# Layer 1's first sum runs behind layer 0's output: the end of a two-layer graph kernel rebuilt

## The chip, the core and the metric

One program runs on one core of a Trainium2 chip. Times are device microseconds (us); the time of the kernel before is the median of three runs, 6874.45 us (6868.21 to 6877.75). One more execution was taken by the profiler, and every line of a profile below comes from that one.

## The reference

Two layers on N = 2708 nodes with 128 features and a dense matrix `adj` (2708 x 2708). Layer 0 is an attention with 128 groups and 8 features in each group: the node matrix `q`, `k`, `v` is read as (128, N, 8), `adj` is added twice to every group's scores, and the softmax goes over the last axis.

```python
a = einsum('dnh,dmh->dnm', q, k) * d ** -0.5
a = softmax(a + adj + adj, axis=2)
out = einsum('dnm,dmh->dnh', a, v).reshape(n, h * d)
x1 = layernorm(x + out @ Wo.T)

local_hidden = adj @ (x1 @ W2) + b2
local_cross = adj @ (local_hidden @ W4) + b4
y = layernorm(x1 + local_cross + local_hidden @ res_w.T + res_b)
```

The `reshape` reads a (128, N, 8) array flat as N rows of 1024 features. 128 rows of the result are therefore 16,384 of the flat (group, node) pairs, some six groups of the attention. The first 128 rows are complete long before the attention ends; only the last ones need its last groups.

## The kernel before

**Attention.** 32 steps of four groups (`GB`), each with six blocks of 452 query nodes (`QB`), each block in nine steps of a `plan`: 1728 steps. TensorE (PE) makes scores and sums weights times values, VectorE (DVE) adds `adj` (L445), ScalarE (ACT) takes exponentials (L536, L539), GpSimd (POOL) multiplies some of them by a stored exponential (L537). A planner, `interleave`, writes the order out by hand. All loads go through SP's DMA queue, eight tiles ahead (`ahead`), from three pools of buffers. `hand_on` (L469 to L471) copies a block's sums out of PSUM and stores them to DRAM (`os`) through the SP queue.

**After it**, `rest(True)` does the remaining work in two stages. A chunk is 128 nodes; there are 22 chunks, the last with 20 nodes. A block is 512 nodes; there are six, the last with 148.

`layer0_out` first loads the weights, then goes over the chunks. Per chunk it loads `ot` (the eight sums and the divisor, 128 x 9 x 128, 576 KB in runs of 512 bytes) and `xt` (the input rows, 64 KB), takes the reciprocal on DVE (L597), notes its smallest and largest value (L600), multiplies (L602), transposes eight 128 x 128 tiles on PE (L605), copies them out on ACT (L607), multiplies them by `wo` (L613, sixteen instructions, since PE makes an f32 product in two passes), and adds `x` with the statistics of the layernorm (L617, L569, L570). `ot` and `xt` have three buffers each; the `xt` of chunk c + 2 waits until chunk c - 1 has been added, and the `ot` of the next chunk stands behind it in SP's queue. After the last chunk, one square root serves all chunks (L632), then every chunk is normalized (L641), transposed (L643) and multiplied by W2 (L651) to give `xw`. A last part, the judgement, checks that sums and exponentials stayed within bounds and puts a number into `n_fine`.

`layer1` runs two passes over the blocks. A pass sums, for each block, 22 products of a chunk of `xw` (then of `hw`) with a 128 x 512 tile of the transposed matrix `adjT`, loaded through SP into 24 buffers (L681, L682). After each block of pass one, the hidden values go to `lhT` (L690) and through W4 to `hw` (L693, L694). After each block of pass two, the residual product is added (L685), the result is transposed, added to `x1`, normalized and stored (L699 to L707).

At the very end the program reads `n_fine`; if the judgement failed, it would do attention and rest again in a slower form. It doesn't here.

[...]A DMA is issued by an instruction on SP's or ACT's queue, and each issue also waits for the DMA that stood eight issues earlier (they share eight completion semaphores).

## Time and profile before

| | us |
|---|---|
| median of three runs | 6874.45 |
| span of the profiled execution, first to last instruction | 6863.4 |
| what lies around the span, by the difference to the median | 11.05 |
| last instruction of the attention's sums on PE ends at | 6522.7 |
| from there to the end | 340.7 |

The profile's own execution is known only by its span. All stages below are read from the span's start. In the stage tables, "busy" is the time in which an engine worked, PEclk the share of full clock that TensorE was granted, and the DMA share the mean busy share of the 16 DMA engines.

### The profile page before, as it was taken

What the parts mean: (1) busy time and instruction counts of PE and PEld (TensorE: products, weight loads), DVE (VectorE), ACT (ScalarE), POOL (GpSimd) and SP (SyncE); (2) the same over time, 40 slices, a digit from 0 to 9 for tenths busy, and PEclk for the clock granted to TensorE, in tenths of its full rate; (3) what the DMA queues carried; (4) which work ended last, traced back from release to release, by engine and by line L of the source; (5) the groups of instructions that cost most, each with busy time, mean ns of one, the idle gap of its engine ahead of it and who ended that gap; (6) DMA issues with size and microseconds to landing.
All of it is one profiled execution on the core that took longest, in us unless ns stands there. A gap on an engine that the chain in (4) does not pass through costs nothing.

```text
span 6863.4 us, 138873 instructions
## 1 busy us (share of the span) xinstructions
PE 6632.4 (97%) x50666; PEld 1992.4 (29%) x50666; DVE 6109.7 (89%) x6373; ACT 6506.3 (95%) x3659; POOL 5788.8 (84%) x2706
## 2 busy tenths in 40 slices
PE   7999999999999999999999999999999999999979
PEld 2222222222222222222222222222222222222254
DVE  6899999999999999999999999999999999999941
ACT  7999999999999999999999999999999999999910
POOL 5899888999988999989889899889999888888800
PEclk8999999999999999999999999999999999999999
DMA  8888888888888888888878778887888787777667
GB/s 263 265 250 248 245 246 249 251 249 247 251 249 248 245 243 247 247 254 254 251 239 249 247 243 250 250 252 242 252 249 244 234 239 235 234 234 231 195 205 232
DMA packets 1168590, 1674.27 MB, mean 244 GB/s; under 512 B 153982, under 2 KB 1135954, under 8 KB 1163802
## 3 DMA queue, kind: packets, MB, share of 16 engines
q1 hardware_dynamic: 1167642, 1664.50, 79.8%
q8 instruction: 402, 6.59, 0.4%
q14 instruction: 290, 2.38, 0.1%
q10 hardware_dynamic: 256, 0.81, 0.1%
HBM read 1582.90 MB, written 81.80 MB: 243 GB/s over the span
## 4 chain that ended last, share of the span: by engine, by line
PE 52%; DMA 12%; DVE 11%; POOL 7%; issue 7%; ACT 6%; SPq 5%; DVEq 0%; POOLq 0%; ACTq 0%
PE acc L463 26%; PE s L438 16%; DVE e L445 9%; POOL w L537 6%; DMA col<-in_adjP 4%; DMA two<-in_adjP 3%; SPq L287 3%; PE acc L682 3%; ACT e L539 3%; ACT w L536 2%; DMA ecol<-ne 2%; PE acc L455 2%; PE p L438 2%; PE s L344 1%; DMA two<-in_adjS 1%
## 5 line engine op out<-in xcount | busy, mean ns | idle before, releaser
L537 POOL TENSOR_TENSOR w<-w,ecol 128x1356 f32<-128x1356 f32 (+1 forms) x1728 | 5347.5, 3102 | 678.8 <-ACT w L536 598.4
L445 DVE TENSOR_TENSOR e<-s,col 128x904 f32<-128x904 f32 (+1 forms) x4608 | 4817.4, 1092 | 306.3 <-PE s L438 68.6
L539 ACT ACTIVATE e<-e 128x2712 f32<-128x2712 f32 (+5 forms) x1728 | 4616.5, 2672 | 17.6 <-DVE e L445 12.0
L463 PE MATMUL acc<-e,vals 128*9 128x452 f32 x20352 | 3554.7, 545 | 0.0
L438 PE MATMUL s<-q,k 32*128 32x452 f32 x10944 | 2492.7, 461 | 122.0 <-DVE e L445 87.7
L536 ACT ACTIVATE w<-p 128x1356 f32<-128x1356 f32 (+1 forms) x1728 | 2308.2, 1336 | 3.0 <-PE p L438 2.5
L438 PEld LDWEIGHTS s<-q,k 32*128 32x128 f32 x10944 | 1002.7, 182 | 3232.8 <-DVE e L445 2845.5
L463 PE MATMUL acc<-w,vals 128*9 128x452 f32 x10368 | 1622.6, 544 | 0.0
L438 PE MATMUL p<-q,k 32*128 32x452 f32 (+1 forms) x5184 | 1322.1, 444 | 25.5 <-ACT w L536 23.1
L445 DVE TENSOR_TENSOR e<-s,two 128x904 f32<-128x904 f32 (+1 forms) x960 | 1049.2, 1093 | 104.5 <-PE s L438 66.0
L463 PEld LDWEIGHTS acc<-e,vals 128*9 128x9 f32 x20352 | 442.3, 88 | 778.0 <-issue 776.5
L438 PEld LDWEIGHTS p<-q,k 32*128 32x128 f32 x5184 | 545.7, 182 | 55.0 <-ACT w L536 47.9
L463 PEld LDWEIGHTS acc<-w,vals 128*9 128x9 f32 x10368 | 209.8, 88 | 176.7 <-issue 159.9
L262 POOL CAST k<-k_raw 128x336 fp32r<-128x336 f32 x251 | 221.6, 883 | 28.2 <-DMA q<-qs 28.2
L460 PE MATMUL acc<-e,v_first 128*32 128x452 f32 (+1 forms) x1536 | 186.7, 558 | 12.8 <-ACT e L539 0.6
L455 PE MATMUL acc<-e,v_short 128*128 128x452 f32 (+1 forms) x384 | 196.7, 594 | 0.0
L344 PE MATMUL s<-wc,xc 128*128 128x256 f32 (+1 forms) x480 | 166.6, 429 | 4.9 <-DMA wc<-in_WqT 0.2
L469 DVE COPY o<-acc 128x452 f32<-128x452 f32 x192 | 120.3, 627 | 51.2 <-PE acc L463 51.2
L360 POOL TENSOR_TENSOR pr<-pa,pr 128x256 fp32r<-128x256 f32 (+1 forms) x160 | 117.5, 734 | 12.8
L346 DVE TENSOR_SCALAR pa<-s 128x256 f32<-128x256 f32 (+1 forms) x240 | 100.4, 419 | 31.1 <-PE s L344 23.7
L344 PEld LDWEIGHTS s<-wc,xc 128*128 128x128 f32 (+1 forms) x480 | 69.5, 183 | 155.0 <-DVE e L445 153.0
L682 PE MATMUL acc<-col,xw 128*128 128x512 f32 (+2 forms) x264 | 105.8, 550 | 0.0
(85 smaller groups left out, 1039.6 us busy)
## 6 DMA issues: line engine op xcount, KB each, us to landing
col<-in_adjP SPq DMA_DIRECT2D x1965, 226.0 KB
two<-in_adjP SPq DMA_DIRECT2D x1440, 226.0 KB
ecol<-ne SPq DMA_DIRECT2D x1395, 226.0 KB
col<-in_adjP SPq DMA_DIRECT2D x393, 224.0 KB
two<-in_adjP SPq DMA_DIRECT2D x288, 224.0 KB
ecol<-ne SPq DMA_DIRECT2D x279, 224.0 KB
col<-in_adjT SPq DMA_DIRECT2D x210, 256.0 KB
k_raw<-ks SPq DMA_DIRECT2D x504, 84.6 KB
```

The lines of the kernel that those rows point to most:

```text
L262: copy(k[:, :, ts(i, n)], t[:, ts(i, n * NU)].rearrange("p (q c) -> p c q", c=NU))
L287: queues[i].dma_start(q[ds(32 * j + 2 * H * i, 2 * H), :nw].bitcast(F32), qs[:, ds((GB * g + j) * N + n0, nw)])
L344: nc.tensor.matmul(pp[:mi, 0, :QW], given[c][:, :mi], given.pop((c, i, h)), start=True, stop=True)
L438: nc.tensor.matmul(to[:, :nw], k[r, m, :], q[r], start=True, stop=True)
L445: nc.vector.tensor_add(e[:, ds(at, 2), :nw], st[:, :, :nw], a)
L455: nc.tensor.matmul(a[:, :nw], vz, e[:, t, :nw], start=False, stop=False)
L460: nc.tensor.matmul(a[ds(32 * j, 32), :nw], v_first[g % 2][:, ds(32 * j, 32)], e[:, t, :nw], start=True, stop=False)
L463: nc.tensor.matmul(a[ds(32 * j, VW), :nw], v[:, m, ds(VW * j, VW)], e[:, t, :nw], start=False, stop=(m == last_chunk))
L536: nc.scalar.activation(w[:, :, :nw], sp[:, :, :nw], AF.Exp, scale=2.0)
L537: nc.gpsimd.tensor_mul(w[:, :, :nw], w[:, :, :nw], exp_cols[g, b, two][:, :nw].unsqueeze(1).to_broadcast([P, 3, nw]))
L539: nc.scalar.activation(e[:, :at, :nw], e[:, :at, :nw], AF.Exp, scale=2.0)
L682: nc.tensor.matmul(acc[:, :nw], src[:mw, m, :], t[:mw, :nw], start=(m == 0), stop=(last is None and m == NM - 1))
```

## The change

The end after the attention is written anew as one function, `finish`; the old form stays only in the part that doesn't run (`again`).

1. Six loads move into the attention: `wo`, the first 128 rows of `adjT` (`near0`), chunk 0's `ot` and `x`, W2 and W4. They are issued on SP's queue at the first six steps of the second block of the last group. The division of chunk 0 (a reciprocal and a multiplication on DVE) goes into the attention's last block.
2. The last store of the attention, and the loads of `rw` and the biases, are issued on ACT's queue.
3. W2 is applied after the sum: adj (x1 W2) becomes (adj x1) W2. Pass one needs only `x1`, so it can start with the first chunk: six accumulators, one for each block, stay open in PSUM, and `spread(c - 2)` adds chunk c - 2 to all six while chunk c is turned and mixed. Each chunk gets its own square root. The rows of `adjT` are loaded whole, 128 x 2708, into six buffers.
4. Two PSUM banks are left for the rest, so transposes are made in two halves through one bank.
5. After the last chunk the sums are taken out, multiplied by W2 (`hidden`) and W4 (`hidden_values`), and pass two (`collect`) begins with the chunks that are ready. Seven of the 22 row chunks are still in SBUF; the other 15 are loaded per block as 128 x 512 tiles into 20 buffers (`fetch`).
6. The output of a block is normalized together (`results`). The judgement runs after the second block of pass two.

```diff
@@ -186,6 +186,15 @@
+    wo = const.tile([P, H, D], F32, name="wo")
+    w2, w4 = (const.tile([P, P], F32, name=f"w{i}") for i in range(2))
+    near0 = const.tile([P, N], F32, name="near0")
+    ot0 = const.tile([P, H + 1, P], F32, name="ot0")
+    x0 = const.tile([P, D], F32, name="x0")
+    o3 = os_.rearrange("e (i g) -> i e g", g=P)
+    early = [(wo.rearrange("g e f -> g (e f)"), WoT), (near0, adjT[:P, :]), (ot0, o3[:P]), (x0, x[:P, :]), (w2, W2), (w4, W4)]
...
@@ -467,8 +476,9 @@
             n0, nw = QBS[b]
             o = opool.tile([P, QB], F32, tag="o", name="o")
             nc.vector.tensor_copy(o[:, :nw], acc.pop((g, b))[:, :nw])
+            queue = nc.scalar if (g, b) == (NG - 1, len(QBS) - 1) else nc.sync
             for j in range(GB):
-                nc.sync.dma_start(os_[:, ds((GB * g + j) * N + n0, nw)], o[ds(32 * j, H + 1), :nw])
+                queue.dma_start(os_[:, ds((GB * g + j) * N + n0, nw)], o[ds(32 * j, H + 1), :nw])
...
@@ -511,6 +521,14 @@
+                if g == NG - 1 and b and early:
+                    nc.sync.dma_start(*early.pop(0))
+                if (g, b) == (NG - 1, len(QBS) - 1) and i in (3, 5):
+                    if i == 3:
+                        quotient = opool.tile([P, QB], F32, tag="o", name="o")[:, :P]
+                        nc.vector.reciprocal(quotient, ot0[:, H, :])
+                    else:
+                        nc.vector.tensor_mul(ot0[:, :H, :], ot0[:, :H, :], quotient.unsqueeze(1).to_broadcast([P, H, P]))
...
-    wo = keep.tile([P, H, D], F32, name="wo")
-    nc.sync.dma_start(wo.rearrange("g e f -> g (e f)"), WoT)
...
-    def layer0_out(sb, ps, pa, judge):
...
-    def layer1(s, cols):
...
+    def finish(s):
+        NR = 6
+        one = s.enter_context(tc.tile_pool(name="one", bufs=1))
+        two = s.enter_context(tc.tile_pool(name="two", bufs=2))
+        sb = s.enter_context(tc.tile_pool(name="end", bufs=3))
+        rpool = s.enter_context(tc.tile_pool(name="rows", bufs=NR))
+        cols = s.enter_context(tc.tile_pool(name="near", bufs=20))
+        turned = s.enter_context(tc.tile_pool(name="turned", bufs=1, space=PSUM))
+        mixed = s.enter_context(tc.tile_pool(name="mixed", bufs=1, space=PSUM))
+        wide = s.enter_context(tc.tile_pool(name="wide", bufs=1, space=PSUM))
+        s.enter_context(tc.manual_schedule())
...
+        given, rows, turns, made, near = {0: (ot0, x0)}, {0: near0}, {}, {}, {}
+        accs = [wide.tile([P, NB], F32, tag=f"acc{k}", name="acc1") for k in range(len(NBS))]
+        def load(c):
+            i0, w = MC[c]
+            ot = sb.tile([P, H + 1, P], F32, tag="ot", name="ot")
+            nc.sync.dma_start(ot[:w], o3[ds(i0, w)])
+            xt = sb.tile([P, D], F32, tag="xt", name="xt", bufs=4)
+            nc.sync.dma_start(xt[:w], x[ds(i0, w), :])
+            given[c] = ot, xt
+        def load_rows(m):
+            m0, mw = MC[m]
+            rows[m] = rpool.tile([P, N], F32, tag="rows", name="rows")
+            nc.sync.dma_start(rows[m][:mw], adjT[ds(m0, mw), :])
+        def divide(c):
+            w, ot = MC[c][1], given[c][0] if c else ot0
+            if c:
+                rd = two.tile([P, P], F32, tag="rd", name="rd")
+                nc.vector.reciprocal(rd[:w], ot[:w, H, :])
+                nc.vector.tensor_mul(ot[:w, :H, :], ot[:w, :H, :], rd[:w].unsqueeze(1).to_broadcast([w, H, P]))
+            for i, op in enumerate((ALU.min, ALU.max)):
+                nc.vector.tensor_reduce(reach[:w, i, c : c + 1], ot[:w, H, :], AX.X, op)
+        def turn(c, h):
+            w, ot = MC[c][1], given[c][0]
+            pt = turned.tile([P, 4, P], F32, tag="pt", name="pt")
+            for e in range(4):
+                nc.tensor.transpose(pt[:, e, :w], ot[:w, 4 * h + e, :], ident[:w, :w])
+            turns[c, h] = two.tile([P, 4, P], F32, tag=f"oT{h}", name="oT")
+            nc.scalar.copy(turns[c, h][:, :, :w], pt[:, :, :w])
+        def mix(c):
+            w = MC[c][1]
+            made[c] = mixed.tile([P, NB], F32, tag="py", name="py")
+            for e in range(H):
+                nc.tensor.matmul(made[c][:w, :D], turns[c, e // 4][:, e % 4, :w], wo[:, e, :], start=(e == 0), stop=(e == H - 1))
+        def add_x(c):
+            w = MC[c][1]
+            y = two.tile([P, D], F32, tag="y", name="y")
+            nc.vector.tensor_add(y[:w], made.pop(c)[:w, :D], given.pop(c)[1][:w])
+            statistics(mvs[:w, c, :], y[:w], w)
+            sd = stat.tile([P, 1], F32, tag="sd", name="sd")
+            nc.scalar.activation(sd[:w], mvs[:w, c, 1:2], AF.Sqrt, bias=eps[:w])
+            rs = stat.tile([P, 1], F32, tag="rs", name="rs")
+            nc.vector.reciprocal(rs[:w], sd[:w])
+            nc.vector.tensor_scalar(x1[:w, c, :], y[:w], mvs[:w, c, 0:1], rs[:w], ALU.subtract, ALU.mult)
+        def spread(m, ks):
+            mw = MC[m][1]
+            for k in ks:
+                n0, nw = NBS[k]
+                nc.tensor.matmul(accs[k][:, :nw], x1[:mw, m, :], rows[m][:mw, ds(n0, nw)], start=(m == 0), stop=(m == NM - 1))
+        NK = len(NBS)
+        resident = {0, *range(NM - NR, NM)}
+        wanted = [(k, m) for k in range(NK) for m in range(NM) if m not in resident]
+        def fetch(n=1):
+            for k, m in wanted[:n]:
+                (n0, nw), (m0, mw) = NBS[k], MC[m]
+                near[k, m] = cols.tile([P, NB], F32, tag="near", name="near")
+                nc.sync.dma_start(near[k, m][:mw, :nw], adjT[ds(m0, mw), ds(n0, nw)])
+            del wanted[:n]
+        for c in (1, 2):
+            load(c)
+            load_rows(c)
+        for t, a in ((rw, res_wT), (b2_sb, b2), (b4_sb, b4), (rb_sb, res_b)):
+            nc.scalar.dma_start(t, a)
+        nrow = 3
+        for c in range(NM):
+            if c + 3 < NM:
+                load(c + 3)
+            while nrow < NM and nrow <= min(c + 4, max(c + NR - 2, NR)):
+                load_rows(nrow)
+                nrow += 1
+            if c == 1:
+                spread(0, range(NK))
+            turn(c, 0)
+            if c > 2:
+                spread(c - 2, range(3))
+            turn(c, 1)
+            if c > 2:
+                spread(c - 2, range(3, NK))
+            mix(c)
+            if c == 0:
+                add_x(0)
+            if c + 1 < NM:
+                divide(c + 1)
+            if c == 0:
+                divide(0)
+            else:
+                add_x(c)
+        fetch(20)
+        nc.vector.tensor_add(bias, b4_sb, rb_sb)
+        spread(NM - 2, range(NK))
...
+        def take(k):
+            nw = NBS[k][1]
+            summed[k] = two.tile([P, NB], F32, tag="summed", name="summed")
+            (nc.vector.tensor_copy if k % 2 else nc.scalar.copy)(summed[k][:, :nw], accs[k][:, :nw])
+        def hidden(k):
+            n0, nw = NBS[k]
+            pl = turned.tile([P, NB], F32, tag="pt", name="pl")
+            nc.tensor.matmul(pl[:, :nw], w2, summed.pop(k)[:, :nw], start=True, stop=True)
+            nc.vector.tensor_scalar(lhT[:, ds(n0, nw)], pl[:, :nw], b2_sb, None, ALU.add)
+        def hidden_values(k):
+            cs = block_chunks[k]
+            ph = mixed.tile([P, 4, P], F32, tag="py", name="ph")
+            for c in cs:
+                m0, mw = MC[c]
+                nc.tensor.matmul(ph[:mw, c - cs[0], :], lhT[:, ds(m0, mw)], w4, start=True, stop=True)
+            full = len([c for c in cs if MC[c][1] == P])
+            nc.scalar.copy(hw[:, ds(cs[0], full), :], ph[:, :full, :])
+            for c in cs[full:]:
+                nc.vector.tensor_copy(hw[: MC[c][1], c, :], ph[: MC[c][1], full, :])
+        def collect(k, ms, first, last):
+            n0, nw = NBS[k]
+            if first:
+                sums2[k] = wide.tile([P, NB], F32, tag=f"acc{NK - 1 - k}", name="acc2")
+            for i, m in enumerate(ms):
+                mw = MC[m][1]
+                t = rows[m][:mw, ds(n0, nw)] if m in resident else near.pop((k, m))[:mw, :nw]
+                nc.tensor.matmul(sums2[k][:, :nw], hw[:mw, m, :], t, start=(first and i == 0), stop=False)
+                fetch()
+            if last:
+                nc.tensor.matmul(sums2[k][:, :nw], rw, lhT[:, ds(n0, nw)], start=False, stop=True)
+        def embed(k):
+            nw = NBS[k][1]
+            embeds[k] = two.tile([P, NB], F32, tag="eT", name="eT")
+            nc.vector.tensor_scalar(embeds[k][:, :nw], sums2.pop(k)[:, :nw], bias, None, ALU.add)
+        def results(k):
+            n0, nw = NBS[k]
+            cs, eT = block_chunks[k], embeds.pop(k)
+            pe = turned.tile([P, 4, P], F32, tag="pt", name="pe")
+            for c in cs:
+                m0, mw = MC[c]
+                nc.tensor.transpose(pe[:mw, c - cs[0], :], eT[:, ds(m0 - n0, mw)], ident)
...
+            for i, n, w in parts:
+                nc.vector.tensor_add(y[:w, ds(i, n), :], pe[:w, ds(i, n), :], x1[:w, ds(cs[0] + i, n), :])
+                for r in range(i, i + n):
+                    statistics(mv[:w, r, :], y[:w, r, :], w)
+                sd, rs = (stat.tile([P, 4], F32, tag=t, name=t) for t in ("sd4", "rs4"))
+                nc.scalar.activation(sd[:w, :n], mv[:w, ds(i, n), 1], AF.Sqrt, bias=eps[:w])
+                nc.vector.reciprocal(rs[:w, :n], sd[:w, :n])
+                for r in range(i, i + n):
+                    nc.vector.tensor_scalar(o[:w, r, :], y[:w, r, :], mv[:w, r, 0:1], rs[:w, r - i : r - i + 1],
+                                            ALU.subtract, ALU.mult)
+                m0 = MC[cs[0] + i][0]
+                nc.sync.dma_start(out[ds(m0, n * w), :].rearrange("(c p) f -> p c f", p=w), o[:w, ds(i, n), :])
+        def judge():
...
+            nc.vector.tensor_reduce(every, fine, AX.X, ALU.min)
...
+            pf = mixed.tile([P, NB], F32, tag="py", name="pf")
+            nc.tensor.matmul(pf[:1, :1], every, ones, start=True, stop=True)
+            nc.vector.tensor_copy(n_fine, pf[:1, :1])
+        spread(NM - 1, [5, 4])
+        take(5)
+        spread(NM - 1, [3])
+        take(4)
+        hidden(5)
+        spread(NM - 1, [2])
+        hidden(4)
+        take(3)
+        spread(NM - 1, [1])
+        hidden_values(5)
+        take(2)
+        spread(NM - 1, [0])
+        hidden_values(4)
+        take(1)
+        order = [*block_chunks[5]]
+        for k in range(3, -1, -1):
+            hidden(k)
+            if k == 1:
+                take(0)
+            collect(0, order, k == 3, False)
+            hidden_values(k)
+            order = [*block_chunks[k + 1]]
+        collect(0, block_chunks[1], False, False)
+        collect(0, block_chunks[0], False, True)
+        embed(0)
+        for k in range(1, NK):
+            collect(k, range(4), True, False)
+            results(k - 1)
+            collect(k, range(4, NM), False, True)
+            embed(k)
+            if k == 1:
+                judge()
+        results(NK - 1)
+    with ExitStack() as s:
+        finish(s)
```

## The prediction

> **What bounds the kernel now.** I first cut the span into stages (busy time by engine), then read the chain that ended last, then the waits of SP's queue. Columns of the stage table: stretch, length, busy time of PE, weight loads, DVE, ACT and POOL, granted clock, DMA share, GB/s.
>
> ```profile
> 6300.00:6520.00 220.00, 207.09 (x1672) 57.85 (x1672) 204.90 (x212) 219.11 (x117) 183.55 (x69) 1.00 0.63 207
> 6522.70:6623.70 101.00, 67.42 (x528) 63.53 (x528) 68.67 (x156) 21.54 (x22) 0.41 (x5) 0.90 0.72 206
> 6623.70:6642.40 18.70, 15.65 (x79) 11.10 (x79) 11.79 (x34) 7.43 (x15) 0.00 (x0) 0.82 0.21 57
> 6642.40:6746.60 104.20, 104.20 (x301) 49.96 (x301) 4.27 (x7) 5.55 (x23) 0.00 (x0) 1.00 0.79 240
> 6746.60:6854.60 108.00, 108.00 (x293) 49.85 (x293) 22.45 (x105) 5.68 (x21) 0.00 (x0) 1.00 0.77 259
> 6854.60:6863.40 8.80, 0.94 (x5) 0.43 (x4) 2.34 (x11) 0.48 (x2) 0.00 (x0) 0.67 0.10 25
> ```
>
> In the attention's last group ACT is busy 219 of 220 us: it sets the pace there. Both passes of layer 1 keep PE busy all the time. Between them and the attention lie 120 us (6522.7 to 6642.4) in which no engine is full. So all that can be gained is in 120 us, about 1.7% of the run.
>
> The chain shows what those 120 us wait for (start, length, what):
>
> ```profile
> 6528.04 4.48 DMA ot<-os
> ...
> 6588.03 0.95 DVE rd L597
> ...
> 6589.31 1.13 DVE on L602
> ...
> 6591.05 4.58 DMA ot<-os
> ...
> 6618.15 0.81 PE pt L605 x8
> 6618.97 3.85 PE py L613 x32
> ...
> 6659.71 0.86 PE acc L682 x2
> ```
>
> Ten microseconds go by between the attention's last sum (6522.7) and the first `ot` (6532.5). Then each chunk costs a load of 4.5 to 5.6 us and some 3 us of DVE, about 7.6 us (6588.03 to the next reciprocal at 6595.65), while the PE needs 0.81 + 3.85/2 = 2.73 us a chunk. SP's waits name the loop: the `xt` load waits for the sums of an older chunk and holds the next `ot` behind it.
>
> ```profile
> SPq L591 <- DVE st L569: 53.3, 19, 4.4
> ```
>
> The chain's last line gives one product of a chunk with a 512-wide block: two passes, 0.86 us.
>
> **The change, part by part.** *PE work* hardly changes. Turn and mix stay at 2.73 us a chunk. Adding a chunk to six sums is 5 x 0.86 + 0.27 (the 148-wide block: 32 instructions took 4.38 us, so 0.27 a pair) = 4.57 us. W2 falls from 22 transposes and 44 products (L643, L651) to five products of 0.86 and one of 0.27, 4.6 us. What changes is that 22 x 4.57 us of pass one lie inside the stage that had holes. If a chunk then costs 2.73 + 4.57 = 7.3 us of PE and nothing else is slower, the stage is PE's.
>
> *Does PE have to wait inside a chunk?* In the built order PE runs: 4 transposes, 3 sums, 4 transposes, 3 sums, 16 mixing products. The second transposes need the one bank copied out by ACT. That copy stands on ACT behind the previous chunk's square root, which waits for DVE: add 0.29, statistics 0.47, root 0.3, copy 0.59 (the 128 x 512 copy at L648), with hops about 1.9 us. PE meanwhile has 0.4 + 2.58 us. The mixing needs the second copy, 0.6 us, behind 1.99 us of sums. DVE per chunk: 0.95 + 1.21 + 0.5 + 0.3 + 0.5 + 0.16 + 0.34 = 4.0 us plus the wait for the root, under 7.3. So none, by about 1 us; if that cover fails, each chunk pays what is missing.
>
> *Do the loads keep up?* A chunk needs 576 + 64 + 1354 KB (128 rows of 10,832 bytes) = 2.04 MB. Nearest rows: 6545 to 6610, mostly `ot`, moved 240 GB/s at a share of 0.82, so 293 when full: 7.0 us. Pass two moved 259 at 0.77, so 336: 6.1 us. [...]The row decides, since a third of the bytes still comes in 512-byte runs: 7.0 us, below 7.3 by little. [...]by the row they set the first four chunks. Below 280 GB/s they set all.
>
> *The start.* ACT's queue now holds, ahead of the first copy of `oT`, eight DMA issues (0.3 to 0.4 us each). They wait for the attention's last sum (6522.7), for DVE's copy (6523.4), and by the shared semaphores for DMAs eight issues back: the fourth store waits for chunk 1's `ot`, issued when POOL ends at 6520.8 and landed 4.5 us later. So the first copy comes at about 6526.4, not 6523.2; queued behind it are all of chunk 0's steps. Then, with hops: copy 0.55, transposes, copy, mixing with a cold clock, add, statistics, root, scale: `x1` of chunk 0 at 6533.6. The timeline shows how PE runs after a hole (start, length of the group, idle time before it in brackets):
>
> ```profile
> 6535.20 1.94 PE L605 MATMUL pt<-ident,on 128*128 128x128 f32 x8 [12.58 <-DVE on L602]
> 6541.43 1.04 PE L605 MATMUL pt<-ident,on 128*128 128x128 f32 x8
> 6550.51 1.94 PE L605 MATMUL pt<-ident,on 128*128 128x128 f32 x8 [2.75 <-DVE on L602]
> ```
>
> Loads come in turn behind each other. The second `ot` waits on a shared semaphore until the first whole row block has landed (6525.5 + 4.5 = 6530), so it lands at about 6534.5; row blocks of about 4.6 us and `ot`s of 2.3 us follow: `ot` 3 at 6541.5, two row blocks, `ot` 4 at 6553.5. Its division takes 2.2 us: chunk 4 starts on PE at about 6556. PE alone would be there at 6553 to 6555, so the loads decide this.
>
> *From there:* 18 chunks x 7.3 = 131.4, less 0.5 for the short last one: 6687. Then two chunks of sums 9.1; W2 4.6; W4 44 products of 0.11 = 4.9; pass two 5 x 23 x 0.86 + 23 x 0.27 = 105.1; transposes of the results 22 x 0.11 = 2.4: together 126.1, to 6813.1. Its tiles: 15 of 22 per block, 3.9 MB in 19.8 us, 200 GB/s against 259 before: hidden, and the first 20 are issued as soon as the last rows are.
>
> *The judgement* moves into pass two. PE's one small product for it stands between the second and third block, and waits for DVE: copy of the sums 0.7, a check on 44 numbers about 0.4, eight small operations and one more 1.4 (6635.95 to 6637.4), hops: PE stands still for 3 us. Queued behind it are the third block's products. SP then reads `n_fine` and holds its loads some 3 us more; by then all 20 buffers are filled, so nothing waits. Does the hole also cool the clock? [...]The third line above shows half speed after 2.75 us of idling, though in a stage with other holes; by that it costs up to 2 more. I take 4.
>
> *In the attention:* the early loads are six issues of about 0.4 us on SP and 2.6 MB, 8 to 9 us of transfer on a share of 0.63; every tile of the second block stands behind them. The table of waits in the last groups shows almost no wait for a load on any engine:
>
> ```profile
> POOL w L537 <- DMA q<-qs: 2.3, 5, 0.5
> ...
> POOL w L537 <- DMA col<-in_adjP: 0.4, 1, 0.4
> ```
>
> Matching issue and first use of each tile, the shortest lead after 6200 is 9.7 us and the median 17, so a delay of 5 is covered; all of it exposed would cost 9. DVE's 0.95 + 1.21 are added at 204.90 busy of 220: 0 to 2.2 us. I take 1 for both. Small waits in the new code: 2. The tail: from the end of PE's last sum to the end of the span was 6863.4 - 6854.6 = 8.8; now DVE also still has the block before to finish: 9.6.
>
> *Sum:* 6813.1 + 1 + 4 + 2 + 9.6 = 6829.7 against 6863.4, that is 33.7 us less, say 34. Against the median: 6874.45 - 34 = 6840, since 11 us around the span stay.
>
> **The rivals.**
>
> *Hidden waits in the chunk.* The margins of about 1 us before the second transposes don't hold, because the chain DVE, ACT, PE crosses three queues. For it: the timeline has hops of 0.1 to 0.2 us between engines, and one late root holds them all. At 0.7 us a chunk: 19 x 0.7 = 13, so 6853.
>
> *The attention pays.* Early loads come in front of its tiles. For it: ACT has no slack (219 of 220), so a late tile is lost time. Against: the leads. At worst 9 + 2.2: 6850.
>
> *Loads keep the pace.* If they stay at the 240 GB/s of the old stage, a chunk costs 8.5 us: 18 x 1.2 + 4 x 1.5 = 28 us of the 34 are lost: 6868, no difference worth naming.
>
> *Slower.* The same place, at a higher price: each `ot` stands on SP's queue behind a row block that waits for a buffer. The gain is gone when 18 (t - 7.3) + 4 (t - 7.0) = 34, so t = 8.8 us a chunk (232 GB/s); it is slower by over 0.2% above 9.4 us. At 10 us: 22 x 10 - 159 = 61 lost, 6901. For it: the old stage moved 206 GB/s on average. Against: it was then SP's waits and not the DMA engines that held it; now an `ot` is asked for three chunks (22 us) ahead.
>
> *Better.* The loads run near 350 GB/s from the start and no clock is lost: 6 to 10 us less, 6832.
>
> **How the numbers follow.** Forecast as worked out (6836 to 6848) 0.56; hidden waits 0.14; the attention pays 0.10; better 0.10; loads keep the pace 0.06; slower 0.04. The range holds the first four: 6828 to 6858, which leaves out 0.10 for the last two and as much for the edges of the others. A difference of 0.2% (13.7 us) is about what a measurement of this kernel can tell from none. Faster: the first four and a third of the fifth, 0.92; same 0.04; slower 0.04.
>
> **What would show it.** Right: the attention's last sum within 2 us of 6522.7; first sum into the accumulators at about 6534, chunk 4 at 6556; from there PE busy all the time with 7.3 us a chunk and clock 1.00; the last sum of pass one near 6700; one hole of 3 us on PE after the second block of pass two; the tail under 10 us. Wrong: a DMA share near 1 with PE below 0.95 in the chunks (loads), transposes waiting for ACT's copy (hidden waits), ACT below 0.99 in the last group (attention).

## The result and the profile after

The changed kernel takes 6854.52 us (median of ten runs, 6848.58 to 6860.71) against 6869.94 us (ten runs of the kernel before, 6865.77 to 6877.75): a ratio of 0.9977, 95% interval 0.9968 to 0.9986. That is 15.4 us less, inside the range on record (6828 to 6858) but less than half of the 34 us forecast; the likeliest case's own range (6836 to 6848) was missed. The profiled span is 6852.6 us, against 6863.4 before: 10.8 us less.

In what follows T0 is the start of the copy of the attention's last sums: 6522.7 before, 6541.05 after. So the attention ended 18.3 us later, and what follows it became 29.1 us shorter (311.6 instead of 340.7). The 18.3 us are 9.4 up to the first block's copy of sums, -1.5 from there to the block before the last group, 3.9 in the next five blocks and 6.6 in the last block.

Two words come back below. A hole is a time in which PE does nothing. A fall is a stretch in which TensorE was granted half of its clock; the trace records the start and length of each.

The stages of the changed kernel, busy time by engine (columns as in the prediction's first table): the attention's last block, the start of `finish`, the chunks, the work up to the second block's end in pass two, the judgement, the rest of pass two, the tail.

```profile
6507.00:6541.00 34.00, 32.36 (x225) 8.12 (x226) 22.69 (x24) 24.42 (x13) 20.77 (x7) 0.80 0.19 59
6541.00:6571.40 30.40, 18.60 (x86) 13.49 (x87) 11.00 (x26) 5.27 (x9) 0.41 (x5) 0.72 0.88 306
6571.40:6708.50 137.10, 137.10 (x685) 89.83 (x683) 68.79 (x167) 25.08 (x57) 0.00 (x0) 1.00 0.80 272
6708.50:6769.70 61.20, 61.15 (x177) 28.41 (x176) 11.49 (x32) 5.35 (x11) 0.00 (x0) 1.00 0.45 134
6769.70:6778.00 8.30, 5.75 (x14) 2.67 (x15) 2.34 (x13) 0.00 (x0) 0.00 (x0) 0.79 0.14 34
6778.00:6842.70 64.70, 64.70 (x190) 31.26 (x188) 16.41 (x59) 1.19 (x4) 0.00 (x0) 1.00 0.43 127
6842.70:6852.60 9.90, 0.46 (x3) 0.15 (x2) 2.77 (x11) 0.59 (x2) 0.00 (x0) 0.61 0.14 42
```

The stage that had holes is PE's now: 137.10 of 137.10 us at full clock with a DMA share of 0.80. Three places are not: the start (18.60 of 30.40), the judgement, and the attention's last block, whose clock fell to 0.80.

The chain that ended last, from the attention's last product on POOL to the first chunk with sums inside (start, length, what):

```profile
6536.01 3.09 POOL w L555
6539.12 4.43 DMA ot<-os
6543.56 5.12 DMA os<-o
6548.71 0.59 ACT oT L636
...
6550.47 3.43 PE py L642 x16
...
6555.91 7.56 PE acc L659 x12
...
6571.35 0.44 PE pt L634 x4
6571.78 2.58 PE acc L659 x6
6574.36 0.44 PE pt L634 x4
6574.80 1.97 PE acc L659 x6
6576.77 1.78 PE py L642 x16
6578.55 0.44 PE pt L634 x4
```

A load, then a store, then the first copy of `oT`, at T0 + 7.7. The chain names the store because it landed last before the copy. What the copy stood behind is seen on ACT's queue:

```profile
6541.05 0.36 ACTq L677 DMA_DIRECT2D rw<-in_res_wT  x1
...
6548.25 0.37 ACTq L677 DMA_DIRECT2D b<-in_res_b  x1
6548.71 0.58 ACT L636 COPY oT<-pt 128x512 f32<-128x512 f32 x1 [10.45 <-DMA os<-o]
```

The last bias waits for the DMA eight issues ahead of it, the load of `rw`: in the trace both tell of their landing by the same one of eight semaphores, and in the profile of before 10,050 of 10,065 issues on SP's queue use the semaphore of the issue eight earlier. By the trace's semaphore records the load of `rw` landed at 6548.23, 7.2 us after its issue; a row block of `adjT`, issued on SP's queue 0.02 us ahead of it, landed at 6548.04. By then the clock is at half (a fall of 17.07 us from 6544.4 on): 3.43 us for the mixing that takes 1.78 later, 7.56 for the first sums instead of 4.55. The last six lines are one chunk as it then repeats: 0.44 + 2.58 + 0.44 + 1.97 + 1.78 = 7.2 us, no idle time between.

SP's waits among the chunks (6560 to 6700):

```profile
SPq L611 <- PE pt L634: 85.1, 18, 6.9
```

An `ot` load now waits for the transposes to free its buffer, that is for PE. Before, it waited for an `xt` load held by the sums.

PE's timeline around the judgement (idle time before the group in brackets):

```profile
6772.25 0.19 PE L792 MATMUL pf<-ones,every 128*1 128x1 f32 x2 [2.60 <-DVE every L789]
6772.37 5.40 PE L741 MATMUL acc<-near,hw 128*128 128x512 f32 x8
```

A hole of 2.6 us, and then eight products in 5.40 us that take 3.60 at full clock (shown below).

### The profile page after: what moved, and what is told of

Its sections match the earlier page's. It is cut to its first block, busy times and chain, and to the rows that moved or that the text cites. A ratio compares the mean times of both kernels' runs of the same rounds, so it can differ in the third digit from the quotient of the medians.

```text
span 6852.6 us, 138413 instructions
## 1 busy us (share of the span) xinstructions
PE 6636.6 (97%) x50612; PEld 1985.7 (29%) x50612; DVE 6114.5 (89%) x6368; ACT 6503.0 (95%) x3660; POOL 5789.9 (84%) x2706
## 4 chain that ended last, share of the span: by engine, by line
PE 51%; DMA 11%; DVE 10%; POOL 9%; issue 7%; ACT 6%; SPq 6%; DVEq 0%; POOLq 0%; ACTq 0%
PE acc L472 25%; PE s L447 16%; DVE e L454 9%; POOL w L555 8%; SPq L296 3%; ACT e L557 3%; DMA col<-in_adjP 3%; DMA two<-in_adjP 3%; ACT w L554 2%; DMA ecol<-ne 2%; PE acc L464 2%; PE p L447 2%; PE acc L659 2%; PE acc L741 2%; PE s L353 1%
## 5 line engine op out<-in xcount | busy, mean ns | idle before, releaser
L659 PE MATMUL acc<-rows,x 128*128 128x512 f32 (+2 forms) x252 | 103.1, 545 | 0.0
```

The lines of the kernel that those rows point to most:

```text
L659: nc.tensor.matmul(accs[k][:, :nw], x1[:mw, m, :], rows[m][:mw, ds(n0, nw)], start=(m == 0), stop=(m == NM - 1))
```

## The experiments

The kernel before was timed again beside each set of runs, with medians of 6865.6 to 6874.5 us. Across sets, therefore, ratios compare better than microseconds.

**Is the late attention a matter of runs?** The copy of sums just before the last group was 7.8 us late already, where nothing had been changed.

> The kernel before, unchanged, profiled once more. The changed kernel's attention ran 7.8 us late already at the end of the block before the last group (6334.05 against 6326.19 for the copy of that block's sums), although the change touches nothing ahead of the last group. If that is a difference from run to run (theory), this profile's copy of the same block may lie anywhere from 6318 to 6342 and the distance from there to the last copy of sums is again 196.5 us to within 1 us. If the change somehow causes it (rival), this profile is within 2 us of 6326.19.

Measured: 6877.72 us, one run. The second profile has this copy at 6338.46, 12 us later than the first and later than the changed kernel's 6334.05. By then its clock had been at half for 27.3 us since block 0, that of the first profile for 3.4. From there to the last copy it takes 199.56 us, not 196.5, with two more falls of 3.4 us each. So the attention as a whole varies by such amounts from run to run, and a single pair of profiles can't tell a few us in it. Its first block is another matter: the first copy of sums stands at 91.19 and 94.43 in the two profiles of before, and at 100.57 after. That is taken up below.

**The division in the last block.**

```diff
             if what == "hand_on":
+                if n == NG * len(QBS) - 1:
+                    quotient = opool.tile([P, QB], F32, tag="o", name="o")[:, :P]
+                    nc.vector.reciprocal(quotient, ot0[:, H, :])
+                    nc.vector.tensor_mul(ot0[:, :H, :], ot0[:, :H, :], quotient.unsqueeze(1).to_broadcast([P, H, P]))
                 hand_on(*divmod(n, len(QBS)))
...
-                if (g, b) == (NG - 1, len(QBS) - 1) and i in (3, 5):
...
```

> The two VectorE instructions that divide chunk 0 (0.94 and 1.22 us) are taken out of the last block and put behind its last addition, ahead of the copy of its sums, where VectorE waits for TensorE anyway. Theory (they stop TensorE, and its clock falls to half afterwards): from the copy of the sums of the last block but one to that of the last takes 27.4 us again as in the kernel before (34.0 in the changed kernel), no slice of the last block has a clock below 0.95, and the whole run is 6 to 7 us shorter than the changed kernel: about 6848, ratio 0.9968 to the kernel before. Rival (the last block suffers from the loads and stores around it): it stays near 34 us with a clock near 0.5 in two stretches, and the time stays at 6854.

Measured: 30.38 us for the last block, 6853.57 us in all (0.9972, 0.9962 to 0.9983). Neither theory's number. One of the two falls of the clock went, the other stayed, behind a hole of 1.06 us that the kernel before has too. The time by itself can't tell this from no change: the interval overlaps that of the changed kernel. The same holds for the experiments on ACT's queue and on the judgement below, which rest on their traces.

The opposite: the division alone, in the kernel before.

```diff
+    ot0 = const.tile([P, H + 1, P], F32, name="ot0")
+    nc.gpsimd.memset(ot0, 1.0)
...
+                if (g, b) == (NG - 1, len(QBS) - 1) and i in (3, 5):
+                    if i == 3:
+                        quotient = opool.tile([P, QB], F32, tag="o", name="o")[:, :P]
+                        nc.vector.reciprocal(quotient, ot0[:, H, :])
+                    else:
+                        nc.vector.tensor_mul(ot0[:, :H, :], ot0[:, :H, :], quotient.unsqueeze(1).to_broadcast([P, H, P]))
```

> The kernel before, with nothing of the change but the two VectorE instructions of the division in the last block, in the same two places, on a tile of ones that nobody reads afterwards (4608 bytes of SBUF in front of the attention's tiles, a multiple of 512). Theory (the two instructions stop TensorE for 0.8 us each, and a stop of 1.9 us at that place brings the clock down): from the copy of the last block but one to the last copy 31 to 34 us, against 27.39 and 27.35 in two profiles of the kernel before, with at least one stretch at half clock. Rival (the clock falls there because of the early loads or by chance): 28 to 29 us and clock 1.00. The first loads of raw keys, by the theory of the tile's place: 10.4 to 11.6 us.

Measured: 31.51 us, one fall; 6876.28 us, one run. The last block by stage, first in the kernel before, then with the division alone in it:

```profile
6495.00:6522.70 27.70, 26.86 (x224) 7.36 (x224) 21.42 (x23) 24.76 (x13) 21.45 (x7) 1.00 0.23 70
```

```profile
6505.80:6537.30 31.50, 29.74 (x224) 7.60 (x224) 22.41 (x24) 24.01 (x13) 20.70 (x7) 0.89 0.19 62
```

And PE's hole in the first, then its two holes in the second:

```profile
6495.47 0.47 PE L438 MATMUL s<-q,k 32*128 32x448 f32 x2 [1.05 <-DVE e L445]
```

```profile
6505.95 0.67 PE L440 MATMUL s<-q,k 32*128 32x448 f32 x2 [1.86 <-DVE e L447]
6516.83 0.47 PE L440 MATMUL s<-q,k 32*128 32x448 f32 x2 [0.80 <-DVE e L447]
```

The 0.94 us reciprocal makes the hole of 1.05 us, which the block has anyway, one of 1.86. Over all profiles of this study the division costs as follows (last copy but one to last copy): in nine profiles with it 31.12 to 33.97 us, each with 6.8 to 13.7 us at half clock; in five without it 27.35, 27.36, 27.39 with none, and 30.17 and 30.38 with 6.8. Means 32.3 and 28.5. So a block without a fall takes 27.4 us, one with a fall and without the division 30.2 to 30.4, one with a fall and the division 31.1 to 32.0, one with two falls and the division 33.9. The longer hole itself is about 1 us of this, and the falls are the rest. The division is not their only cause, since two of the five blocks without it had one as well. Nor is the longest hole always the one: in two of the nine profiles the fall came 9 us after it, behind holes of 0.7 and 0.5 us.

The last group is where falls come anyway. In the five blocks ahead of the last, the 14 profiles have 27 falls in 70 blocks, the three without early loads among them 4 in 15; in the 185 blocks before those, 27 in 2590. PE is busy 94% of the time there (149.78 of 160 us from 6340 on in the kernel before), against 98% at 3000 to 3200. No run tests whether this is the reason.

**The loads on ACT's queue.**

```diff
-        for t, a in ((rw, res_wT), (b2_sb, b2), (b4_sb, b4), (rb_sb, res_b)):
-            nc.scalar.dma_start(t, a)
...
         assert nrow == NM
+        for t, a in ((rw, res_wT), (b2_sb, b2), (b4_sb, b4), (rb_sb, res_b)):
+            nc.sync.dma_start(t, a)
         fetch(20)
```

> The four loads of the residual weights and the biases leave ScalarE's queue and go on SP's, behind the last row block. Theory (they hold the first copy of oT, since the last of them waits on a shared semaphore for a store of sums): the first copy of oT comes 3 us after the last copy of sums began (7.7 in the changed kernel), when the fourth store is issued; the hole of TensorE shrinks from 7.8 to about 3.5 us, and the first chunk with sums inside begins 25 to 27 us after the end of the attention instead of 30.3; the run is 4 us shorter, about 6850, ratio 0.9972. Rival (the start is set by the loads of the chunks 1 to 3, as the prediction's sum had it): the first copy comes sooner but that chunk still begins 30 us after the end, and the time stays at 6854. A half way between says that both hold.

Measured: 6850.72 us (0.9970, 0.9959 to 0.9981). The first copy of `oT` comes 0.53 us after T0, sooner than expected, since it now stands ahead of the four stores on ACT's queue; the timeline of ACT:

```profile
6548.35 0.59 ACT L636 COPY oT<-pt 128x512 f32<-128x512 f32 x1 [3.29 <-PE pt L634]
6548.48 1.49 ACTq L481 DMA_DIRECT2D os<-o  x4
6550.01 0.59 ACT L636 COPY oT<-pt 128x512 f32<-128x512 f32 x1 [1.07 <-DMA os<-o]
```

So the copy doesn't need the stores; it only stood behind them. Chunk 3, the first with sums inside, begins at T0 + 20.4 instead of T0 + 30.3, and between T0 and there the chain that ended last has PE, ACT and DVE in it and no load. So the loads of the chunks did not set the start; the queue did. The edit moves the stores behind the copy too, so it doesn't tell the share of the four loads from that of the stores; by the trace above the wait for `rw` alone held the queue from 6544.26 to 6548.25. Yet from T0 to the end only 4.1 us are gained (307.45 against 311.56): 4.4 are given back around the last chunk's sums, where the clock fell to half for 10.24 us, and 1.3 at the judgement, where it fell for 6.8 us instead of 3.4.

**The judgement's product.** The DVE part stays; the product on PE goes behind the next four products.

```diff
...
             collect(k, range(4), True, False)
+            if k == 2:
+                ask()
             results(k - 1)
             collect(k, range(4, NM), False, True)
             embed(k)
             if k == 1:
-                judge()
+                ask = judge()
```

> The one small product by which the sums are judged is moved on TensorE's queue behind the first four products of the third block of pass two; VectorE's part of the judgement stays where it was. Theory: the hole of 2.8 us at the second block's end and the half-speed products behind it (5.33 us for eight instead of 3.43) both go, unless the product moved waits itself: its result takes about 2.8 us from the end of the second block and the four products last 3.4 us, so it does not; from the end of pass one's sums to the last sum of pass two 129.5 us instead of 134.2, the run 4.7 us shorter, about 6850. Rival (the clock falls for another reason there[...]): only the hole goes, 2.8 us, and a stretch at half clock stays.

Measured: 6850.48 us (0.9971, 0.9959 to 0.9983). From the first product of pass two to its last 115.7 us instead of 120.1: 4.4 us less. PE's timeline there:

```profile
6770.94 1.12 PE L744 MATMUL acc<-lhT,rw 128*128 128x512 f32 x2
6771.90 3.60 PE L741 MATMUL acc<-near,hw 128*128 128x512 f32 x8
6775.43 0.19 PE L794 MATMUL pf<-ones,every 128*1 128x1 f32 x2
```

The hole and the half clock behind it are gone together.

**The place of the tiles.** Every profile of a changed kernel started late. The new tiles stand ahead of the attention's in SBUF; `near0` has 2708 elements a partition, and pushes the raw keys' tile from byte 26624 of a partition to 47712.

```diff
-    near0 = const.tile([P, N], F32, name="near0")
+    near0 = const.tile([P, 2816], F32, name="near0")
...
```

> One size is changed: the early row block's tile gets 2816 elements a partition instead of 2708, so that the new tiles push every tile of the attention by a multiple of 512 bytes (the raw keys' tile starts at byte 48128 of a partition instead of 47712; in the kernel before at 26624). Four profiles of changed kernels issue the first 16 loads of raw keys in 14.1 to 15.0 us and copy the first block's sums at 98.8 to 100.6; two of the kernel before need 10.4 and 11.5 us and stand at 91.2 and 94.4. Theory (the place of the tile in SBUF makes the 10832-byte packets slow, 1055 to 1141 ns against 726 and 837): the loads take 10.4 to 11.6 us again, packets of 720 to 840 ns, the first block's sums at 91 to 95, and the run is some 6 us shorter than the changed kernel, 6848. Rival (the longer program or something else at the start does it): 14 to 15 us and 98.8 to 100.6 again, time 6854.

Measured: 6848.3 us (0.9960, 0.9946 to 0.9974). The issue of SP's half of these loads and the first copy of sums, in the changed kernel and then with the padded tile:

```profile
16.00 14.95 SPq L263 DMA_DIRECT2D k_raw<-ks  x8
100.57 0.62 DVE L478 COPY o<-acc 128x452 f32<-128x452 f32 x1
```

```profile
15.89 10.61 SPq L263 DMA_DIRECT2D k_raw<-ks  x8
92.97 0.62 DVE L478 COPY o<-acc 128x452 f32<-128x452 f32 x1
```

The 128 packets of the 16 loads (10,832 bytes each, one row of a partition) take 785 ns instead of 1170. A multiple of 64 bytes (2736 elements) was tried too:

> The changed kernel with the early row block's tile at 2736 elements a partition: the raw keys' tile starts at byte 47808, a multiple of 64 but not of 128 (47712, a multiple of 32 only, in the changed kernel; 48128 with the tile of 2816 elements; 26624 before). If a multiple of 64 is enough: first 16 loads of raw keys 10.4 to 12.1 us, their packets 720 to 905 ns, the first block's sums at 91 to 95. If it takes more than 64: 13.6 us or more, 950 ns or more, 98.5 or later. A value between would say that the place counts by degrees.

Measured: 15.13 us, 1196 ns, first copy at 103.47. So a multiple of 64 wasn't enough here. Over all 14 profiles: with the tile at a multiple of 512 bytes the first copy stands at 91.19 to 94.83 (six profiles, mean 93.4), elsewhere at 98.53 to 103.47 (eight, mean 100.5). This is 7.1 us that no part of the change asked for. Multiples of 128 and 256 weren't tried. At the other places the packets took 34% more than at a multiple of 512 (means of the profiles 1131 and 843 ns). Why they do, and why this group of loads is hit so hard, stays open: from 500 to 6300 us packets of this size take 605 ns before and 609 after.

**The early loads.**

```diff
-                if g == NG - 1 and b and early:
+                if g == NG - 1 and b and i % 4 == 0 and early:
```

> The six early loads go out one in four steps of the last group's second and third block instead of one a step in the second. In the changed kernel the two copies of sums around them came 1.6 and 1.5 us late (33.85 us a block in the quiet blocks ahead), in three other profiles between 3 and 9 us were lost from there to the last block but one. Theory (2.6 MB in six steps delays the attention's tiles): from the end of the block before the last group to the last block but one 169 to 170.5 us, against 173.04 in the changed kernel and 169.14 before. Rival (what is lost there are falls of the clock that come by chance): 172 us or more, with stretches at half clock where no early load is near.

Measured: 176.05 us from the block before the last group to the last but one, where the unspaced loads took 173.04: no gain, with 13.7 us at half clock in that stretch. One run at 6863.03 us tells no more. The comparison over all profiles does: without early loads this stretch took 169.14 us with no half clock, 172.21 with 6.8 us of it, 174.49 with 10.2 (the division alone in the kernel before). With early loads it took 169.93 with none, 172.13 to 173.04 with 6.8 to 7.3 us, 173.75 with 10.2, 176.05 with 13.7, 177.52 with 17.1. The two rows lie on one line to within 0.8 us, near 169.2 plus half of the time at half clock. The early loads have no cost of their own above that. Whether they make the falls more frequent can't be told from three profiles without them.

**How fast can the loads be?**

```diff
             turn(c, 1)
-            if c > 2:
+            if c > 2 and c - 2 in (1, NM - 3):
                 spread(c - 2, range(3, NK))
```

> The changed kernel without the last three of the six sums in all chunks but the first two and one near the end (so the output is not the reference's): a chunk's work on TensorE falls from 7.2 to 0.44 + 2.58 + 0.44 + 1.78 = 5.24 us, while its loads stay at 2.04 MB. What a chunk then takes tells how fast the loads can be: 7.0 us if they run at 293 GB/s, as the rows of the old stage had it (the value that the prediction took), [...]5.5 at the 371 that stretches of these profiles show, and 5.24 if they are still hidden. The rival of the prediction that loads keep the pace at 240 GB/s asks for 8.5 us.

Measured: 5.34 us a chunk (6822.92 us, one run). The chain that ended last:

```profile
6595.74 0.44 PE pt L634 x4
6596.18 1.89 PE py L642 x16
6598.07 0.44 PE pt L634 x4
6598.50 2.58 PE acc L659 x6
6601.08 0.44 PE pt L634 x4
```

PE still sets the pace, and the loads follow, as the stage table of the same kernel shows:

```profile
6590.00:6610.00 20.00, 20.00 (x118) 14.72 (x117) 13.69 (x35) 4.99 (x12) 0.00 (x0) 1.00 1.07 375
```

375 GB/s at a share of 1.07 (in this view the share can pass 1): at 7.2 us a chunk the loads had a margin of at least 1.9 us. The floor itself wasn't reached.

**All together**, with the four last stores on POOL's queue too (all are shown above but this):

```diff
-            queue = nc.scalar if (g, b) == (NG - 1, len(QBS) - 1) else nc.sync
+            queue = nc.gpsimd if (g, b) == (NG - 1, len(QBS) - 1) else nc.sync
```

> All corrections at once: the division behind the last addition, the four loads of weights and biases on SP's queue behind the last row block, the last block's four stores on GpSimd's queue instead of ScalarE's, the early loads one in four steps, the product of the judgement four products later, and the tile of 2816 elements. If each is worth what it is by itself and they add: 6 (start) + 3 (clock and division in the last block) + 3 (early loads) + 4 to 9 (first copy of oT) + 4.7 (judgement) = 21 to 26 us less than the changed kernel, 6829 to 6834, ratio 0.9940 to 0.9947. If the start of layer 0's output is set by loads and the clock falls elsewhere instead: 12 to 15 less, 6840, ratio 0.9955.

Measured: 6833.28 us, ratio 0.9934 (0.9921 to 0.9948): 21 us under the changed kernel's median, and 26 if each is set against the kernel before of its own set (41.2 less instead of 15.4). That is the size that was forecast for the sum, though 3 us of the sum stood for early loads that show no cost. The stages of this kernel: the last block, the start, the chunks, then the last chunk's sums with W2 and the start of pass two.

```profile
6506.00:6534.00 28.00, 27.15 (x228) 7.77 (x228) 26.65 (x26) 24.85 (x13) 21.76 (x12) 1.00 0.24 74
6534.00:6552.40 18.40, 13.71 (x87) 10.38 (x86) 11.06 (x26) 5.27 (x9) 2.45 (x7) 1.00 1.05 382
6552.40:6690.00 137.60, 137.60 (x684) 90.10 (x683) 69.36 (x169) 25.07 (x57) 0.00 (x0) 1.00 0.83 287
6690.00:6709.00 19.00, 19.00 (x43) 7.91 (x42) 3.57 (x10) 2.22 (x5) 0.00 (x0) 0.73 0.00 1
```

The last block takes 27.36 us at full clock, the start 18.4 instead of 30.3, and from T0 to the end it is 299.8 us against 311.6. The last row is odd: PE busy 19.00 of 19.00 and yet a clock of 0.73. There the last chunk's products, which sum over 20 rows, are issued.

> The kernel with all corrections, and one thing more: the sums of the last chunk (20 rows) are no longer issued one after another behind those of the chunk before it, but in turn with them, block by block, so that the copies and W2 of the small blocks begin sooner and products over 128 rows stand between those over 20. In three of seven profiles (the kernel with all corrections among them) the clock fell to half for 10.24 us at this place, though TensorE's records show no hole there; in four it did not. Theory[...]: no fall at this place, and from the end of the attention to its end 295 us where that kernel had 299.83; median 6828 to 6830. Rival (it falls by chance, or for the short waits in that stretch): a fall of 6.8 or 10.24 us here too, 300 us, median 6833.

```diff
-        spread(NM - 2, range(NK))
+        spread(NM - 2, [5, 4, 3])
...
-        spread(NM - 1, [5, 4])
+        spread(NM - 1, [5])
         take(5)
-        spread(NM - 1, [3])
+        spread(NM - 2, [2])
+        spread(NM - 1, [4])
         take(4)
         hidden(5)
-        spread(NM - 1, [2])
+        spread(NM - 2, [1])
+        spread(NM - 1, [3])
...
```

Measured: 6828.35 us, ratio 0.9943 (0.9930 to 0.9957), which is not to be told from the 0.9934 before it. The fall was one of 3.41 us instead of 10.24, and from T0 to the end it took 298.44 us, not 295. A fall at the start took 1.7 us of this; from chunk 4 to PE's last product it is 2.8 us less. That is part of the expected effect, in one profile. Whether products over 20 rows bring the clock down is not shown by it. Of ten profiles with the old order five have a fall of 10.24 us there, one a fall of 3.41 and four none.

**The changed kernel once more.**

> The changed kernel, unchanged, profiled once more. If the place of the raw keys' tile sets the start: first 16 loads of raw keys 13.6 to 15 us, first block's sums at 98.5 to 100.6. If the division stops TensorE: from the last block but one to the last copy 31 to 34 us with at least one stretch at half clock. If the start of layer 0's output hangs on the last load on ScalarE's queue: the first copy of oT 7.2 to 8.1 us after the copy of sums. Against these: one that falls outside.

Measured: 6856.45 us, one run; 14.64 us for the loads, first sums at 101.96 (a little outside the stated 100.6, on the far side from before's), last block 33.92 us with two falls, first copy at T0 + 7.87. The three costs repeat. From T0 to the end it took 314.36 us, 2.8 more than in the first profile, with a fall of 10.24 us at the last chunk's sums.

## Why the prediction was right, and where it was not

The direction was right, and so was the reason for it: the stage that had holes is full, at 7.2 us a chunk. The size was too large. That the time still lies in the stated range is in part luck, since the range was that wide for rivals whose reasons did not come true.

In spans: 33.7 us were forecast and 10.8 came. The 22.9 us between are 17.3 in the attention, 4.2 in the start, 1.1 from there to the last product and 0.3 in the tail.

*What bounds the kernel; PE in the chunks.* Right. 7.2 us a chunk for 7.3, no waits inside, from chunk 4 to PE's last product 264.1 us where the sum has 263.1. The rivals "hidden waits" and "loads keep the pace", and with them "slower", fell here: PE has no idle time between the chunk's pieces.

*Do the loads keep up?* The conclusion was right, the term was mis-sized. I took 293 GB/s, from a row whose stage waited for something else, against the 336 of pass two. The experiment with half of the sums moves 375, more than either, and a stretch inside pass two of the kernel before (6745 to 6765) moved 384. The rate divided by the share, read in a stage that did not wait for its loads alone, gave 293, less than the loads moved there.

*The start.* "The first copy comes at about 6526.4" was T0 + 3.7 and measured 7.7: I followed ACT's queue to the fourth store's wait, and stopped there. The eighth issue, the last bias, waits for a DMA eight issues back in turn, the load of `rw` at the head of the same queue, which took 7.2 us to land. "The loads decide this" was wrong as well: with the queue clear, chunk 3 begins 9.9 us sooner on the same loads of `ot` and rows. The two errors partly met: chunk 4 came 4.2 us late. "Loads come in turn" is what the trace of before shows: the first three `ot`s, issued on SP's queue at 6528.04, 6529.18 and 6531.20, landed at 6532.52, 6534.78 and 6536.98, each `xt` between them 0.2 us behind its `ot`.

*In the attention, "I take 1 for both".* This step failed, at two places. The division was put at 0 to 2.2 us, the busy time it adds; it cost about 5 over the kernel before (32.3 against 27.4 us), up to 6.6, and 3.8 over the mean of the five blocks without it (28.5). About 1 us is the longer hole on PE; the rest is half clock behind the holes, which came in nine of nine blocks with the division and in two of five without. For the judgement I had weighed whether a hole brings the clock down (the row had half speed after 2.75 us), and I had not asked it of the attention. Here falls came behind holes of 1.86, 1.06 and even 0.7 us. The early loads, which I had bounded at 9, show no cost. "The attention pays" was the right rival by size, but for neither reason it gave: not a late tile, and not the 2.2 us.

*What was missing.* The 7.1 us at the start of the run, from new tiles that push old ones to other addresses. No step of the prediction looked at it. With the means of all profiles (7.1; 3.9 more for the division, from 27.4; the 4.2 and 1.4 of the first profile) the sum gives 17 us less instead of 33.7, near the 15.4 of the medians.

*The judgement.* 4 taken, 4.4 measured by the experiment that removes it; the row of the trace (up to 2 us more than the hole) gave the right size. *The tail*: 9.6 taken, 9.9 measured.

*"11 us around the span stay."* Wrong as a statement: 1.8 us lie around the changed kernel's span (6854.41 less 6852.6) and 2.1 around the second profile of before. So the profiled execution of before took about 6865.5 by that, quicker than the median. Only the difference of spans carried the forecast, so nothing followed from it.

## What to carry to other kernels

Two VectorE instructions of 0.94 and 1.22 us cost about 4 to 5 here (a block of 32.3 us on average with them, 28.5 without, 27.4 in the kernel before), although VectorE had time to spare (21.42 of 27.70 us busy in the kernel before), because TensorE waited for VectorE there: its hole of 1.05 us became one of 1.86, and the block had half clock in nine of nine profiles with the division. Follow a queue with shared completion semaphores to its last issue before the instruction that matters, and keep small loads that nobody needs yet off it: here the wait for `rw` held ACT's queue from 6544.26 to 6548.25. New long-lived tiles ahead of old ones are worth padding: with a multiple of 512 bytes a partition, the only step that helped here, the first sums were copied at 93.4 us on average, elsewhere at 100.5. And the start of the run should be compared even where the change is at its end.

## What the runs showed of the hardware

Falls of the clock lasted 3.41 us or a multiple of it, in all 14 profiles (6.83, 10.24, 13.65, 17.07 and, near the start of the run, up to 37.55), but for the one that the end of the run cuts off. They came behind a hole of 1.06 us in two of five profiles. A fall of 10.24 us also came in five of ten profiles with no hole over 0.1 us in TensorE's records, where products run over 20 rows. SBUF loads of 10,832-byte rows on two queues at once took 34% longer (1131 against 843 ns a packet) with the tile at byte 47712 or 47808 of a partition than at a multiple of 512. The first three chunks of the kernel with all corrections moved 382 GB/s over 18.4 us on one core.
